# A causal attention loop on one core: how the row maxima are formed, and where projection work stands between scores and products

## The chip, the cores and the metric

The kernel runs on one core of a Trainium2 chip. The metric is the device time of one execution in microseconds. TensorE is written PE (matmuls) and PEld (weight loads), VectorE DVE, ScalarE ACT, GpSimd POOL, and SyncE SP; in this kernel SP issues nearly all DMA transfers. [...]

## The reference, cut to what matters

The program is a decoder of two layers on 8 sequences of 256 tokens with 512 features. Six sublayers follow each other, each added to its input and normalised. Three of the six are causal attentions over 256 tokens, and only those are touched here:

```python
# first sublayer: "a", differential attention, 32 query heads of 16, 8 key heads, 4 value heads of 32
scores = einsum('bhqd,bhkd->bhqk', q, k) * HD ** (-0.5)
scores = where(causal, scores, finfo.min)
attn_out = einsum('bhqk,bhkd->bhqd', softmax(scores), v)
lambda_full = exp(sum(lambda_q1 * lambda_k1)) - exp(sum(lambda_q2 * lambda_k2)) + LAMBDA_INIT
attn = attn_out[:, 0::2] - lambda_full * attn_out[:, 1::2]
attn = attn * rsqrt(mean(attn * attn, -1) + EPS) * ln_w * (1 - LAMBDA_INIT)
return attn @ Wo.T
# fourth sublayer: "s", causal self attention, 16 heads of 32
# sixth sublayer: "r", causal attention, 16 query heads of 32, one key and one value of 32 per token,
#                 chosen by the largest of 16 gates
```

Between them lie a long convolution and a mixture of experts (after a), and a cross attention (between s and r). The softmax subtracts each row's maximum before the exponential.

## The kernel before, in words

All three attentions run through one function, `causal_attention`, with `prepare` (projections for a group of four token tiles) and `finish` (output projection, sum and norm of two token tiles) given by the caller. Inside it the order of PE, DVE, ACT and POOL instructions is the order in which the Python code emits them. PSUM tiles and SBUF tiles come from pools; a tile that is asked for again waits until the old contents were read.

The work is cut into slots `u`. A slot handles four heads of one sequence (32 rows of the PE array each); a sequence has 8 slots in a (`upb` = 8) and 4 in s and r, so a has 64 slots, s and r have 32 each. A slot's data passes three stages at different times:

- `maxima(u)`: twelve score matmuls (`ps_q`, L1140), three 128x128 blocks for each of four heads: queries 0 with keys 0, queries 1 with keys 0, queries 1 with keys 1. ACT copies the two diagonal blocks to SBUF (`diag`, L1149). DVE reduces the block below the diagonal straight out of PSUM (`neg`, L1151). POOL masks the diagonal blocks (L1153). A second DVE reduction over `diag` (L1162) is returned as a function and emitted later in the slot. After the last slot of a sequence `split` (L1169 to L1176) writes the maxima as three bf16 terms, and one slot later `turn` (L1184) transposes them on PE and ACT copies them (`negT`, L1192).
- `weights(u - upb)`: the transposed scores less the maxima (`ps_k`, L1205 and L1214), the exponential on ACT (`pT`, L1222), the mask on POOL (L1223) and POOL's sum of two blocks (L1233).
- `products(u - lag)` with `lag = upb + 1`, called by `sums(u)`: weights times values (`ps_pv`, L1248), their sums by a matmul with ones (L1258), reciprocal and product on DVE (L1266, L1272). In a, `gather` takes the place of L1272: even slots multiply (L367), odd slots use `nlam`, the negated lambda (L370), and POOL adds the two (`yT_b`, L371).

So `products` in slot u uses the weights made in slot u - 1. The scores and the transposed scores share one PSUM tile of four banks (`ps_sc`, one buffer). `ps_pv` has one buffer as well, and three one-bank tiles (tag "mm") serve all other matmuls.

Projection work fills PE's gaps. `prepare` puts pieces into `queue`, each step with a cost (0.86 for a matmul group `MM`, 0.45 for a transpose group `TR`) and each piece with the slot at which it is due. `finish` puts pieces into `after`. `fill(budget)` emits steps until less than 0.3 of the budget is left; `need(u)` emits all that is due by slot u, whatever it costs. Every slot has two fills, a short one and the rest. `at` also registers small things for a later slot's "start", "mid" or "end". Before, a slot's order is:

```python
diagonal = maxima(u)
...            # turn of the sequence before, in its first slot
sums(u)
diagonal()
...            # split, "mid" events, short fill
if u >= upb:
    weights(u - upb)
left = fill(left + rate - short)
```

In a, `finish` also normalises each head: squares on ACT (L462), sums on PE (`norms`, L436), then the power -1/2 on POOL over 128x16 (L446), widening on ACT (`widen`, L444), a transpose on PE (`scaled`, L453), a product on DVE (L459) and the output projection (`out_tile`, which ends in `add_norm_later`: sum L211 and statistics L145, L146 on DVE, `rstd` L140, L141 on POOL, and the last product L154 in a later slot). In s, the tokens of the next group come from the experts' sum (`combine`: L1066, L1075) and are normalised by "mid" events.

At the start of a, SP issues: four token tiles, the weights, the other twelve token tiles, four transfers of `filters` (10 MB, for the convolution), then `ln_w` (`lnw`, four times) and the four lambda vectors (`lv`), then the zero fills of two arrays in DRAM. DVE scales `wo` by `lnw` (L278) and forms `nlam` (L291 to L296).

Of the kernel before, what the change touches and what calls it, by code (L numbers as in the profile page):

```python
# [16 lines left out]
F32 = mybir.dt.float32  # L17
# [6 lines left out]
P = 128  # L24
# [25 lines left out]
def decoder_kernel(ctx: ExitStack, tc: tile.TileContext, a: dict, out: bass.AP):  # L50
# [184 lines left out]
    def diff_attention():  # L235
# [11 lines left out]
        for t in range(4):  # L247
            nc.sync.dma_start(
                out=wo[32 * t : 32 * t + 32],
                in_=a["L0_attn_Wo"][P * t : P * (t + 1), :].rearrange("(k d) c -> d k c", d=32),  # L250
            )
        load_x(range(TPG, NT))
# [22 lines left out]
        lnw = const.tile([P, 1], F32, tag="lnw", name="lnw")  # L275
        for i in range(4):
            nc.sync.dma_start(out=lnw[32 * i : 32 * (i + 1), :], in_=a["L0_attn_ln_w"].unsqueeze(1))
# [4 lines left out]
        lv = const.tile([P, 4, HD0], F32, tag="lv", name="lv")  # L282
        for i, n in enumerate(("q1", "k1", "q2", "k2")):
            nc.sync.dma_start(
                out=lv[:, i, :],
                in_=a[f"L0_attn_lambda_{n}"].unsqueeze(0).broadcast_to([P, HD0]),
            )
# [137 lines left out]
        def finish(work, pools, t0, yT, at):  # L425

            cost = 2 * (0.4 + TR + KB * MM)
            if t0 == NT - 2:
                return cost
            wide = {}  # L430
            sq = squares(t0 // 2)

            def norms(i):
                ps = pools.tile([P, H0], F32, tag="mm", name="ps_ss")
                for k in range(KB):
                    nc.tensor.matmul(  # L436
                        ps[:, 4 * k : 4 * k + 4], lhsT=sq[:, k, i * P : (i + 1) * P], rhs=quad, start=True, stop=True
                    )
# [7 lines left out]
                at(0, "end", lambda: nc.gpsimd.tensor_tensor(rr, rr, neg_half, ALU.pow))  # L446
                at(1, "end", widen)
                at(2, "fill", [(TR, lambda: scaled(i))])
# [14 lines left out]
            for i in range(2):  # L463
                at(1 + i, "fill", [(0.4, lambda i=i: norms(i))])
# [621 lines left out]
    def causal_attention(name, prepare, finish, upb=KB, gather=None):  # L1086
# [18 lines left out]
        with ExitStack() as st:  # L1105
# [26 lines left out]
            def maxima(u):  # L1132
# [4 lines left out]
                for j, (i, keys) in enumerate(((0, 0), (1, 0), (1, 1))):  # L1137
# [10 lines left out]
                d = work.tile([P, 4, 2, P], F32, tag="diag", name="diag")  # L1148
                nc.scalar.copy(d, block[:, :, 0:3:2, :])  # L1149
                dst = neg[u // upb % 2][:, :, :, c]  # L1150
                nc.vector.tensor_reduce(dst[:, 1], block[:, :, 1, :], AX.X, ALU.max, negate=True)  # L1151
                rows = d.rearrange("p s j k -> p (s j) k")
# [10 lines left out]
                    dst[:, 0:3:2].rearrange("p j s -> p s j"), d, AX.X, ALU.max, negate=True  # L1163
# [173 lines left out]
            for u in range(units + lag + 2):  # L1337
# [499 lines left out]
```

## Time and profile before

| | |
|---|---|
| median of 3 runs | 2288.14 us (2285.28 to 2297.55) |
| profiled execution, its time | 2304.89 us |
| profiled execution, span from first to last instruction | 2303.1 us |
| mean granted TensorE clock | 0.957 |
| PE, DVE, POOL, ACT busy | 2078.3, 1282.2, 814.5, 545.9 us |
| scores of a, first to last | 21.2 to 486.0 us |
| scores of s and r, first to last | 1229.1 to 2259.4 us |

The views used below come from this one execution. A row of a timeline has the start and the duration in us, the engine, the source line, the operation with out<-in and its shape; in square brackets stands the idle time of the engine before it and what ended it. In a row of waits stand the waiting instruction, what it waited for, the total in us, the number of times and the longest. A row of groups ends in total busy time, mean ns of one, and idle time before it.

### The profile page before, as it was taken

The numbers are of one execution on the slowest core, as the hardware profiler recorded it, in microseconds if no ns is written. First come the engines' busy times: TensorE is split into PE (matmuls) and PEld (weight loads), VectorE is DVE, ScalarE is ACT, GpSimd is POOL, SyncE is SP. The second block draws the span as 40 slices with busy tenths as digits, with TensorE's granted clock in tenths as the row PEclk, the third lists the DMA queues.
The fourth block names the chain that finished last, engine by engine and source line by source line (L and its number), as shares of the span: only waits on it lengthen the run. The fifth ranks groups of instructions, "written<-read, shape, count | busy, mean of one in ns | idle before, by whom it ended". The sixth has DMA issues, their size and how long they took to land. (4 is left out here: it accounts for less than half of the span.)

```text
span 2303.1 us, 35720 instructions
## 1 busy us (share of the span) xinstructions
PE 2078.3 (90%) x14904; PEld 1200.5 (52%) x14904; DVE 1282.2 (56%) x2051; ACT 545.9 (24%) x723; POOL 814.5 (35%) x904
## 2 busy tenths in 40 slices
PE   7688888888999999899978999998999999999995
PEld 4344444544445346555543444444877876545443
DVE  3556666665888895122224556456343433577767
ACT  3334334431001003211112333331101101233322
POOL 2456556564654843000013444334000000133433
PEclk9899989989999999999988999999999999999998
DMA  7899601312413306213122111002001000000000
GB/s 241 307 384 384 240 2 38 98 45 55 179 28 114 115 23 222 80 62 135 60 108 76 38 37 56 19 1 93 28 10 37 28 10 1 1 10 10 15 15 29
DMA packets 110033, 197.57 MB, mean 86 GB/s; under 512 B 7088, under 2 KB 30768, under 8 KB 109872
## 3 DMA queue, kind: packets, MB, share of 16 engines
q1 hardware_dynamic: 104752, 178.49, 22.3%
q0 software_dynamic: 5120, 16.78, 2.2%
q8 instruction: 120, 1.97, 0.3%
q14 instruction: 41, 0.34, 0.0%
HBM read 93.54 MB, written 112.20 MB: 89 GB/s over the span
## 5 line engine op out<-in xcount | busy, mean ns | idle before, releaser
L171 PE MATMUL ps_y<-kv,wt 128*128 128x512 f32 x640 | 281.0, 597 | 4.6 <-POOL kv L508 3.7
L1222 ACT ACTIVATE pT<-ps_k 128x1536 f32<-128x1536 f32 x128 | 185.8, 1451 | 360.4 <-PE ps_k L1214 352.7
L1266 DVE RECIPROCAL rsum<-ps_pv 128x256 f32<-128x256 f32 x128 | 224.3, 1753 | 73.3 <-PE ps_pv L1258 73.3
L1151 DVE TENSOR_REDUCE neg<-ps_q 128x4 f32<-128x512 f32 x128 | 88.4, 691 | 311.7 <-ACT diag L1149 311.6
L1223 POOL TENSOR_SCALAR_AFFINE_SELECT pT<-pT 128x1024 f32<-128x1024 f32 x128 | 140.2, 1095 | 275.4 <-ACT pT L1222 275.1
L1153 POOL TENSOR_SCALAR_AFFINE_SELECT diag<-diag 128x1024 f32<-128x1024 f32 x128 | 140.0, 1094 | 186.3 <-ACT diag L1149 186.2
L171 PEld LDWEIGHTS ps_y<-kv,wt 128*128 128x128 f32 x640 | 120.2, 191 | 153.7 <-issue 135.7
L1149 ACT COPY diag<-ps_q 128x1024 f32<-128x1024 f32 x128 | 129.7, 1013 | 188.8 <-PE ps_q L1140 171.0
L1162 DVE TENSOR_REDUCE neg<-diag 128x8 f32<-128x1024 f32 x128 | 155.3, 1213 | 26.1 <-POOL diag L1153 26.0
L1233 POOL TENSOR_TENSOR pT<-pT 128x512 f32<-128x512 f32 x112 | 142.6, 1274 | 9.3
L140 POOL TENSOR_SCALAR rstd<-bn_mv 128x1 f32<-128x1 f32 x80 | 16.9, 211 | 322.1 <-DVE bn_mv L146 317.8
L1066 POOL DMA_INDIRECT w_l1x<-ys,slots x32 | 31.5, 983 | 280.2 <-DMA ys<-y_m 272.2
L182 PE MATMUL ps_f<-xT,w_l1a 128*128 128x512 f32 x256 | 121.1, 617 | 3.0 <-ACT xT L195 3.0
L182 PE MATMUL ps_t<-w_l1f,xT 128*128 128x512 f32 x256 | 121.5, 613 | 1.4 <-DVE sel L1654 1.4
L981 PE MATMUL po_m<-dn,hT 128*128 (+1 forms) x216 | 104.4, 621 | 12.0 <-ACT hT L974 10.5
L1258 PE MATMUL ps_pv<-pT,ones_v 128*32 128x256 f32 (+1 forms) x1152 | 88.9, 392 | 22.7 <-POOL pT L1233 22.4
L546 DVE TENSOR_REDUCE yc<-z 128x64 f32<-128x512 f32 x128 | 86.1, 674 | 6.1 <-POOL w_l1a L547 5.7
L1248 PE MATMUL ps_pv<-pT,v 128*32 128x256 f32 (+1 forms) x1024 | 60.0, 356 | 30.1 <-POOL pT L1223 29.4
L1205 PE MATMUL ps_k<-qT,kz 32*128 32x256 f32 (+1 forms) x1024 | 75.4, 382 | 4.5 <-DVE neg L1151 4.2
L1140 PEld LDWEIGHTS ps_q<-kT,qT 32*128 32x128 f32 x1536 | 49.2, 188 | 57.3 <-issue 31.6
L1140 PEld LDWEIGHTS ps_q<-kz,qT 32*128 32x128 f32 x1536 | 49.9, 190 | 55.7 <-ACT pT L1222 35.1
L182 PEld LDWEIGHTS ps_f<-xT,w_l1a 128*128 128x128 f32 x256 | 47.3, 194 | 59.5 <-issue 54.8
(327 smaller groups left out, 3763.8 us busy)
## 6 DMA issues: line engine op xcount, KB each, us to landing
xs<-zero SPq DMA_DIRECT2D x8, 4352.0 KB
ys<-zero SPq DMA_DIRECT2D x8, 4352.0 KB
filters<-in_L_xattn_k SPq DMA_DIRECT2D x4, 2560.0 KB
first_h<-xs SPq DMA_DIRECT2D x36, 256.0 KB
ys<-y_m SPq DMA_DIRECT2D x36, 256.0 KB
gu<-in_L_ffn_gate_up_proj SPq DMA_DIRECT2D x3, 2816.0 KB
wt<-filters SPq DMA_DIRECT2D x32, 256.0 KB
x<-in_x SPq DMA_DIRECT2D x16, 256.0 KB
```

Source lines behind the costliest of these rows:

```text
L171: nc.tensor.matmul(ps, lhsT=lhsT(k), rhs=rhs(k), start=(k == 0), stop=(k == n - 1))
L182: nc.tensor.matmul(ps[0], lhsT=lhsT(k), rhs=rhs(k), start=(k == 0), stop=(k == KB - 1))
L981: nc.tensor.matmul(po, lhsT=hT[:m, i, :], rhs=dn[i][:m, bass.ds(e, 1), :], start=(i == 0), stop=(i == len(FCH) - 1),)
L1140: nc.tensor.matmul(block[:, s, j, :], lhsT=q(rows, c, b * S + i * P, P), rhs=k(rows, c, b * S + keys * P, P), start=True, stop=True,)
L1149: nc.scalar.copy(d, block[:, :, 0:3:2, :])
L1153: nc.gpsimd.affine_select(out=rows, in_=rows, compare_op=ALU.is_ge, fill=-FAR, base=0, pattern=[[0, 8], [-1, P]], channel_multiplier=1,)
L1162: return lambda: nc.vector.tensor_reduce(dst[:, 0:3:2].rearrange("p j s -> p s j"), d, AX.X, ALU.max, negate=True)
L1222: nc.scalar.activation(p[:, 0:3].rearrange("p j s q -> p s j q"), block, AF.Exp)
L1223: nc.gpsimd.affine_select(out=p[:, 0:2].rearrange("p j s q -> p (j s) q"), in_=p[:, 0:2].rearrange("p j s q -> p (j s) q"), compare_op=ALU ...
L1233: nc.gpsimd.tensor_tensor(p[:, 3], p[:, 1], p[:, 2], ALU.add)
L1258: nc.tensor.matmul(ps[32 * s : 32 * s + 32, 1, j * P :], lhsT=ones_v, rhs=p[:, 1, s, :] if j else first[:, :, s, :], start=(j == 0), stop= ...
L1266: nc.vector.reciprocal(r, ps[:, 1, :])
```

## The change

It has five parts.

1. In `maxima`, ACT copies all three blocks to SBUF (`rows`, 128x1536), ordered so that the two diagonal ones lie together; POOL masks those two as before; one DVE reduction over all three is emitted later in the slot. The reduction out of PSUM is gone. The tile has two buffers in a and one in s and r (`diag` had two everywhere).
2. The short fill moves up: it now stands right after the scores, before `turn`, the products and the reduction.
3. The rest of the fill stops one `MM` early; then `need(u + 1)` emits what is due in the next slot; then the last step follows.
4. In a, the power over 16 columns is cut into two over 8, emitted at the ends of two slots; the second tile's `norms` comes two slots after the first's, and `widen` and `scaled` move accordingly. In the last-but-one sequence they stay as close as before.
5. The transfers of `lnw` and `lv` are issued before the twelve token tiles and the filters. The turn of the last sequence comes after the products of the following slot.

```diff
+        lnw = const.tile([P, 1], F32, tag="lnw", name="lnw")
+        for i in range(4):
+            nc.sync.dma_start(out=lnw[32 * i : 32 * (i + 1), :], in_=a["L0_attn_ln_w"].unsqueeze(1))
+        lv = const.tile([P, 4, HD0], F32, tag="lv", name="lv")
...
         load_x(range(TPG, NT))
         spread_filters()
...
-        lnw = const.tile([P, 1], F32, tag="lnw", name="lnw")
...
+            apart = 1 if t0 == NT - 4 else 2
...
-                at(0, "end", lambda: nc.gpsimd.tensor_tensor(rr, rr, neg_half, ALU.pow))
-                at(1, "end", widen)
-                at(2, "fill", [(TR, lambda: scaled(i))])
+                def root(half):
+                    r = rr[:, 8 * half : 8 * half + 8]
+                    nc.gpsimd.tensor_tensor(r, r, neg_half[:, :8], ALU.pow)
+
+                for half in range(2):
+                    at(half * (apart - 1), "end", lambda half=half: root(half))
+                at(apart, "end", widen)
+                at(apart + 1, "fill", [(TR, lambda: scaled(i))])
...
-                at(1 + i, "fill", [(0.4, lambda i=i: norms(i))])
+                at(1 + apart * i, "fill", [(0.4, lambda i=i: norms(i))])
...
-                for j, (i, keys) in enumerate(((0, 0), (1, 0), (1, 1))):
+                for j, (i, keys) in enumerate(((0, 0), (1, 1), (1, 0))):
...
-                d = work.tile([P, 4, 2, P], F32, tag="diag", name="diag")
-                nc.scalar.copy(d, block[:, :, 0:3:2, :])
-                dst = neg[u // upb % 2][:, :, :, c]
-                nc.vector.tensor_reduce(dst[:, 1], block[:, :, 1, :], AX.X, ALU.max, negate=True)
-                rows = d.rearrange("p s j k -> p (s j) k")
+                d = work.tile([P, 3, 4, P], F32, tag="rows", name="rows", bufs=2 if gather else 1)
+                nc.scalar.copy(d.rearrange("p j s k -> p s j k"), block)
+                rows = d[:, 0:2].rearrange("p j s k -> p (j s) k")
...
                 return lambda: nc.vector.tensor_reduce(
-                    dst[:, 0:3:2].rearrange("p j s -> p s j"), d, AX.X, ALU.max, negate=True
+                    neg[u // upb % 2][:, :, :, c], d, AX.X, ALU.max, negate=True
                 )
...
                 if u >= units:
 
+                    if u == units:
+                        sums(u)
+                        turn(B - 1)
                     if u < units + upb:
                         weights(u - upb)
-                    sums(u)
+                    if u > units:
+                        sums(u)
...
-                diagonal = maxima(u)
-                if u and u % upb == 0:
-                    turn(u // upb - 1)
-                sums(u)
-                diagonal()
-                if u % upb == upb - 1:
-                    split(u // upb)
-                happen("mid")
+                largest = maxima(u)
                 if u % upg == upb and u // upg + 1 < NG:
                     per_group = begin(u // upg + 1)
                 short = min(0.3 * rate, 0.8)
                 if rate > 2.7:
                     short += (rate - 2.7) / 2
                 left = fill(left + short)
+                if u and u % upb == 0:
+                    turn(u // upb - 1)
+                sums(u)
+                largest()
+                if u % upb == upb - 1:
+                    split(u // upb)
+                happen("mid")
                 if u >= upb:
                     weights(u - upb)
-                left = fill(left + rate - short)
-                if u == units - 1:
-                    turn(u // upb)
+                left = fill(left + rate - short - MM)
+
+                need(u + 1)
+                left = fill(left + MM)
                 happen("end")
```

More of the change, by code (lines that the diff above doesn't have):

```diff
@@ L251, in diff_attention @@
             )
+        lnw = const.tile([P, 1], F32, tag="lnw", name="lnw")
+        for i in range(4):
+            nc.sync.dma_start(out=lnw[32 * i : 32 * (i + 1), :], in_=a["L0_attn_ln_w"].unsqueeze(1))
+        lv = const.tile([P, 4, HD0], F32, tag="lv", name="lv")
+        for i, n in enumerate(("q1", "k1", "q2", "k2")):
+            nc.sync.dma_start(
+                out=lv[:, i, :],
+                in_=a[f"L0_attn_lambda_{n}"].unsqueeze(0).broadcast_to([P, HD0]),
+            )
         load_x(range(TPG, NT))
@@ L273, in diff_attention @@
         nc.vector.tensor_reduce(quad, ident.rearrange("p (t d) -> p t d", t=4), AX.X, ALU.add)
-        lnw = const.tile([P, 1], F32, tag="lnw", name="lnw")
-        for i in range(4):
-            nc.sync.dma_start(out=lnw[32 * i : 32 * (i + 1), :], in_=a["L0_attn_ln_w"].unsqueeze(1))
         nc.vector.tensor_scalar(
@@ L280, in diff_attention @@
         )
[L282 to L287, printed above, removed]
         lam = const.tile([P, 4], F32, tag="lam", name="lam")
```

## The prediction

> **What bounds the kernel now.** I read the page first, for the busiest engine and its clock.
>
> ```profile
> PE 2078.3 (90%) x14904; PEld 1200.5 (52%) x14904; DVE 1282.2 (56%) x2051; ACT 545.9 (24%) x723; POOL 814.5 (35%) x904
> ...
> PEclk9899989989999999999988999999999999999998
> ```
>
> TensorE (PE) is busy for 2078 of 2303 us, so time is won where PE stands still or runs at a lowered clock. Next the stretches of the three causal attentions (columns: length, then busy time and count of PE, PEld, DVE, ACT, POOL, then granted clock, DMA share, GB/s). I call them a (64 slots), s and r (32 slots each).
>
> ```profile
> 88.00:485.00 397.00, 338.69 (x4262) 192.15 (x4260) 253.67 (x308) 163.31 (x172) 234.83 (x213) 0.93 0.56 199
> ...
> 1229.00:1555.00 326.00, 307.53 (x2580) 149.51 (x2580) 178.43 (x262) 106.11 (x124) 138.66 (x154) 0.99 0.11 33
> ...
> 1967.00:2259.00 292.00, 274.25 (x2616) 145.30 (x2620) 203.14 (x305) 89.23 (x98) 104.01 (x108) 0.98 0.03 10
> ```
>
> In a, PE idles 58 us of 397 and its clock is 0.93; in s and r it idles 18 us each at almost full clock. So most of the room is in a. Third, PE's own waits over the whole run (us in total, times, longest):
>
> ```profile
> PE ps_pv L1248 <- POOL pT L1223: 47.3, 34, 11.5
> PE ps_n L1184 <- DVE terms L1173: 28.4, 11, 4.8
> PE ps_pv L1258 <- POOL pT L1233: 22.4, 47, 0.6
> ...
> PE ps_q L1140 <- ACT kT L1387: 7.6, 11, 0.7
> PE ps_k L1205 <- DVE neg L1151: 6.5, 9, 1.9
> ```
>
> The change aims at these five. A slot of a in the timeline shows the first and the third:
>
> ```profile
> 100.11 1.45 ACT L1222 ACTIVATE pT<-ps_k 128x1536 f32<-128x1536 f32 x1 [3.77 <-PE ps_k L1214]
> ...
> 101.61 0.95 PE L1140 MATMUL ps_q<-kz,qT 32*128 32x128 f32 x24 [0.57 <-ACT pT L1222]
> 101.62 1.09 POOL L1223 TENSOR_SCALAR_AFFINE_SELECT pT<-pT 128x1024 f32<-128x1024 f32 x1 [3.38 <-ACT pT L1222]
> ...
> 102.77 0.86 PE L1248 MATMUL ps_pv<-pT,v 128*32 128x256 f32 x16 [0.21 <-POOL pT L1223]
> ...
> 104.12 0.64 PE L1258 MATMUL ps_pv<-pT,ones_v 128*32 128x256 f32 x8 [0.50 <-POOL pT L1233]
> ```
>
> Products of slot u use the weights of slot u-1: exponential, POOL's select, POOL's add. Only the scores stand between, so PE waits 0.21 and 0.50.
>
> **The change, part by part.** Each sum is made on the profiled execution (2304.9 us; median of the runs 2288.1).
>
> *Lambda first.* The only long stall:
>
> ```profile
> 77.45 1.29 DVE L278 TENSOR_SCALAR w_l<-w_l,lnw 128x2048 f32<-128x2048 f32 x1 [9.25 <-DMA lv<-in_L_attn_lambda_q]
> ...
> 82.51 1.51 PE L1248 MATMUL ps_pv<-pT,v 128*32 128x256 f32 x16 [11.47 <-POOL pT L1223]
> ```
>
> DVE stands behind eight tiny transfers queued after the 10 MB of filters; POOL's add and select stand behind DVE, PE behind POOL. Moved ahead of 12 token loads, they land long before DVE's first reduction at 23 us. Gone: 11.47 us and the slow matmuls after it (1.51 for 0.86, 1.08 for 0.64, 1.24 for 0.71 and so on, 2.1 us). Late next: the usual 0.21 and 0.50. Net 12.9. On SP's queue eight issues of about 0.43 us delay the later token loads by 3.5 us; they are issued by 20.7 us and first turned at 52.3 us, so that costs nothing. The zero fills behind them start some 20 us earlier; the next load that a waits for is issued at 246 us.
>
> *A projection piece between scores and products.* The compiled order shows a piece there in 41 of a's slots 9 to 63 (in none before; it stood after the products), and in nearly every slot of s and r. A piece is 0.93 us on PE (1.98 for two), more than 0.21+0.50. The short waits of those 41 slots add up to 13.6 us in the PE timeline. On odd slots POOL first does `yT_b` (0.73), which waits for reciprocal 1.76 and L370 0.48, so a little returns: I take 11. The 14 slots without a piece keep theirs.
>
> In r the waits are 1.5 to 3.2 us long and have another cause:
>
> ```profile
> 2134.47 1.10 POOL L1223 TENSOR_SCALAR_AFFINE_SELECT pT<-pT 128x1024 f32<-128x1024 f32 x1
> ...
> 2135.62 0.86 PE L1248 MATMUL ps_pv<-pT,v_r 128*32 128x256 f32 x16 [1.46 <-POOL pT L1223]
> ```
>
> The exponential was over at 2131.2. POOL's queue held two `rstd` pairs first (to 2134.5), and these waited for DVE's residual and statistics, which stood behind reciprocal and reduction. These residuals come from an output piece in the short fill. Moved ahead of the products, that fill puts residual, statistics and `rstd` ahead of the reciprocal. I take all 11.2 us of r's waits, and the slow spell after the 3.21 one (2.2): 13.4. In s the norm is added by the "mid" event, still after products and reduction, so there the 1.76 and its like stay, 0.5 longer by the bigger reduction: 1 us lost.
>
> *Roots in halves.* L446 takes 2.92 us, L387 on half the columns 1.64. Two of L446 in a row:
>
> ```profile
> 141.97 5.83 POOL L446 TENSOR_TENSOR rr<-rr,neg_half 128x16 f32<-128x16 f32 x2
> ...
> 149.95 0.86 PE L1248 MATMUL ps_pv<-pT,v 128*32 128x256 f32 x16 [2.12 <-POOL pT L1223]
> ...
> 153.86 1.24 PE L1205 MATMUL ps_k<-qT,kz 32*128 32x256 f32 x8
> ```
>
> Four such waits in a: 2.12, 2.14, 2.65, 1.27, together 8.2. In halves, at most 3.3 us fall between two slots and a piece covers 0.93; one us stays, 7.2 gained. POOL pays 14 x (2 x 1.64 - 2.92) = 5 us of its own time, beside PE. After three of them matmuls run slow: the slots' PE time exceeds that of like slots by 2.0, 2.0 and 4.5, so 8.5 more. [...] The row above shows 1.24 us for what takes 0.71, 4 us after a gap of 2.12. I take the row[...].
>
> *All maxima to SBUF.*
>
> ```profile
> L1162 DVE TENSOR_REDUCE neg<-diag 128x8 f32<-128x1024 f32 x128 | 155.3, 1213 | 26.1 <-POOL diag L1153 26.0
> ...
> L1149 ACT COPY diag<-ps_q 128x1024 f32<-128x1024 f32 x128 | 129.7, 1013 | 188.8 <-PE ps_q L1140 171.0
> ...
> L1151 DVE TENSOR_REDUCE neg<-ps_q 128x4 f32<-128x512 f32 x128 | 88.4, 691 | 311.7 <-ACT diag L1149 311.6
> ```
>
> The copy grows by half; L1222 moves the same 1536 columns in the same layout in 1.45, so +0.44 a slot, 56 us on ACT (24% busy). One reduction takes the place of two: 512 columns more cost 1213-691, so 1.74 for 1.90, 21 us less on DVE. Score PSUM is now freed by the copy, at 1.07+1.45 = 2.5 us after the scores' start. The transposed scores (`ps_k`) come after 0.95+0.86+0.57 = 2.4 us, or 3.3 with a piece. So the 6.5 us of L1205 on `neg` go, 0.5 stays: 6.0. If that cover went, the copy would cost up to 128 x 0.44 = 56. I take nothing.
>
> *Due pieces a product ahead.* `ps_q` waits 7.6, 3.7 and 2.9 us for ACT's evacuations of kT and qT, 0.7 each time. A piece of 0.93 now stands between. I take 10 of 14.2; the cost of more reordering is nothing PE must do twice.
>
> *The turn after fill and, at the end, after products.* In a the turn waits for a chain on DVE: reciprocal, product, reduction, then six split operations. Rows show 0.18 to 0.23 us for these, or about 1.0 to 1.3 while POOL works. [...] So hiding 0.93 of the wait would by PE's order alone gain some 6 us in a's six inner turns. [...] it now starts a piece later and is 0.52 longer. For slot 39-40: the transposed scores came 11.9 us after slot 39's scores, and come at about 12.3. I take 0.4 x 6 = 2.5 lost. At the ends the last turn moves behind ready products (1.5 to 2.5 us of PE work): of the waits 2.82, 3.05 and 4.85 I take 8 back. Net 5.5.
>
> **Sum:** 12.9 + 11 + 13.4 - 1 + 7.2 + 8.5 + 6.0 + 10 + 5.5 = 73.5 us. From the profiled 2304.9 that makes 2231; the profiled execution lies 16.8 above the median, most likely in slow spells, so against the median: 2288.1 - 73 = 2215. About 45 of it is in a.
>
> **The rivals.** (0.5%, 11.4 us, is about what a measurement of this kernel tells from no change.)
>
> *The loop stays the bound* (smaller gain). From `ps_k`'s end, exponential 1.6, select 1.1, add 1.3, ones 0.6 and `ps_k` 1.1 make 5.7 us a slot against 6.4 of PE work; queues behind `yT_b` or the norms could close that gap, and then the pieces only change place. Only lambda, roots without spells, `neg` and half the due pieces count: 12.9+7.2+6+5 = 31, so 2257. For it: 14 slots without a piece. Against it: slots with four matmul records of fill already wait for the add alone.
>
> *Full clock in a* (larger gain). At 0.93 over 397 us, 28 us of clock are missing there; I counted 10.6 of a's spells and leave the turns' (about 10). If the shorter gaps end these too, 90 to 105: 2190.
>
> *The single rows buffer* (slower). In s and r the tile has one buffer (before: two): the copy of slot u+1 waits for slot u's reduction, `ps_k` behind the copy, and PE behind that. In r at 2133 the reduction ended at 2141.0 and the next copy began at 2146.0: 5.0 us of room. The bigger reduction takes 0.5 of it and the pieces ahead of the reciprocal 2.8, so 1.6 is left. Where DVE runs later than that, each us is PE's. It turns the 73 into a loss from 2.8 us a slot over 64 slots (room 1.6, then 1.2 x 64 = 74); at 3.5 it is 2288 - 73 + 122 = 2337. Against it: before, `ps_k` waited for a reduction of its own slot, which is later in DVE's order.
>
> *It does not do what it says*: pieces run out and PE has the old order. The compiled order excludes it for s and r.
>
> **How the numbers follow.** My sum 0.63 (2185 to 2240), the loop 0.17 (2240 to 2270), full clock 0.09, no measurable change 0.07, slower 0.04. The range 2178 to 2258 leaves out about 0.2: the end of the larger gain, and those near or above no change. Faster 0.89, same 0.07, slower 0.04.
>
> **What would show it.** The 11.47 wait gone; PE on POOL's `pT` from 69.7 us to under 30; `ps_k` on `neg` and `ps_q` on kT near zero; the turn's wait still near 20 us; the copy at 1.45, the reduction at 1.74; clock in a 0.95 or more. Wrong if PE's waits for `pT` stay above 45, if `ps_k` waits for the copy, or if a shortens by less than 25 us.

## The result, and the profile after

The changed kernel takes 2255.53 us (median of 4 runs, 2248.47 to 2261.73) against 2287.40 us (4 runs, 2285.28 to 2297.55): a ratio of 0.985, 95% interval 0.9814 to 0.9885 (ratios here are of the means, the times are medians). It is 32 us faster; the sum had forecast 73. The profiled execution took 2256.86 us. Its page (engine, busy time, share of the span, instructions; then the granted clock in 40 slices):

```profile
PE 2072.2 (92%) x14904; PEld 1204.6 (53%) x14904; DVE 1272.1 (56%) x1923; ACT 600.0 (27%) x723; POOL 820.2 (36%) x918
...
PEclk8999999798999999999979999989999999998898
```

PE is as busy as before (2072 us): what went is idle time. Look also at the end of the clock row, where r lies: it shows two 8s in a row, where before there were only 9s until the last slice. PE's waits over the whole run (total us, times, longest):

```profile
PE ps_pv L1254 <- POOL pT L1229: 18.6, 17, 2.7
PE ps_n L1190 <- DVE terms L1179: 14.1, 8, 2.7
...
PE ps_pv L1264 <- POOL pT L1239: 9.9, 23, 0.8
PE ps_o L182 <- DVE yT_b L467: 9.3, 4, 4.3
...
PE pt_k L1681 <- DVE k L1676: 4.6, 2, 2.3
...
PE ps_n L1190 <- DVE sel L1665: 3.0, 1, 3.0
PE pt L194 <- DVE sel L1665: 2.7, 1, 2.7
```

By the waits alone the forecast looks met. Those for POOL's `pT` fell from 69.7 us to 18.6 + 9.9 = 28.5; `ps_k` on `neg` is gone, `ps_q` on kT and qT is down to three waits of 0.7 us; the copy takes 1.44 us and the reduction 1.75, as said (the whole-run rows of groups):

```profile
L1168 DVE TENSOR_REDUCE neg<-rows 128x12 f32<-128x1536 f32 x128 | 223.5, 1746 | 64.9 <-POOL rows L1159 64.9
L1157 ACT COPY rows<-ps_q 128x1536 f32<-128x1536 f32 x128 | 184.1, 1438 | 182.8 <-PE ps_q L1148 153.6 <-DVE neg L1168 17.7 <-DVE v_r L1671 4.3
```

But the table of waits shows new names too: `sel`, `k`, and `yT_b` of the output projection. And the windows of a, s and r (length, then busy and count of PE, PEld, DVE, ACT, POOL, then clock, DMA share, GB/s) show where the time did not come:

```profile
88.00:440.00 352.00, 305.55 (x4056) 179.64 (x4056) 233.83 (x246) 176.07 (x163) 228.64 (x214) 0.96 0.62 221
1177.00:1500.00 323.00, 306.11 (x2553) 148.84 (x2552) 175.95 (x227) 118.30 (x123) 137.33 (x153) 0.98 0.11 34
1914.00:2214.00 300.00, 285.79 (x2642) 155.23 (x2641) 203.84 (x275) 103.53 (x99) 105.28 (x108) 0.94 0.03 10
```

In a the clock rose from 0.93 to 0.96 and the idle time fell from 58 to 46 us. The window of r is 300 us long instead of 292 (from the first scores to the last 297 against 292): idle fell from 18 to 14, but the clock fell from 0.98 to 0.94.

To compare kernels I cut each profile at fixed marks. "a" runs from the first `ps_q` to the convolution's first `ps_y`, s from its first `ps_q` to the cross attention's first `ps_x`, r from that attention's last `ps_x` to the end. The last column adds up, in slices of 1 us from r's first scores to its last, how far the granted clock lay under 1 (slices under 0.9 only): time at half clock counts half.

| kernel (us) | a | s | r | r's clock loss |
|---|---|---|---|---|
| before, two profiles | 543.8, 546.5 | 411.1, 410.2 | 404.3, 407.6 | 6.8, 10.1 |
| changed, three profiles | 504.6, 503.9, 504.5 | 414.7, 413.9, 417.4 | 404.2, 403.1, 403.2 | 18.6, 15.2, 15.2 |
| E1 ahead in a alone | 504.0 | 417.1 | 406.7 | 12.0 |
| E2 fill behind | 533.9 | 417.4 | 406.6 | 11.9 |
| E3 old maxima | 497.9 | 407.6 | 399.9 | 8.4 |
| E4 due late | 498.5 | 413.9 | 400.4 | 10.1 |
| E6 old maxima, due late | 496.5 | 410.2 | 411.2 | 20.3 |
| E7 lambda late | 521.0 | 414.5 | 403.2 | 15.1 |
| E8 whole roots | 507.7 | 410.9 | 402.3 | 13.5 |
| E9 turn ahead in s, r | 500.4 | 430.2 | 399.2 | 8.5 |
| E10 three edits | 496.8 | 418.3 | 406.6 | 11.9 |
| E11 turn first | 509.0 | 413.0 | 402.5 | 15.4 |
| E13 double rows | 503.5 | 417.6 | 405.8 | 15.2 |
| E14 best | 497.6 | 411.3 | 402.9 | 10.0 |
| E15 order alone | 507.6 | 408.6 | 411.8 | 17.0 |

So a gave 39 us (the sum had about 45 there), s lost 3 to 7 and r gave next to nothing, where the sum had 7 or 8 and some 20. In a, about half of the gain is clock: from the first scores to the last PE idles 56.5 us instead of 79.6, and its clock loses 20.5 us instead of 39.3 (35.8 in the second profile of before). A part of the profiles' difference, 47.9 us in the spans, is not the change's: the experts' stage between convolution and s took 362.8 us in the profile of before and 350.4 in that after. E12 below settles that.

### The profile page after: what moved, and what is told of

The parts are those of the page before. It is cut to its first block, busy times and chain, and to the rows that moved or that the text cites. A ratio compares the mean times of both kernels' runs of the same rounds, so it can differ in the third digit from the quotient of the medians.

```text
span 2255.2 us, 35573 instructions
## 1 busy us (share of the span) xinstructions
PE 2072.2 (92%) x14904; PEld 1204.6 (53%) x14904; DVE 1272.1 (56%) x1923; ACT 600.0 (27%) x723; POOL 820.2 (36%) x918
## 3 DMA queue, kind: packets, MB, share of 16 engines
q8 instruction: 120, 1.97, 0.4%
## 5 line engine op out<-in xcount | busy, mean ns | idle before, releaser
L1168 DVE TENSOR_REDUCE neg<-rows 128x12 f32<-128x1536 f32 x128 | 223.5, 1746 | 64.9 <-POOL rows L1159 64.9
L1157 ACT COPY rows<-ps_q 128x1536 f32<-128x1536 f32 x128 | 184.1, 1438 | 182.8 <-PE ps_q L1148 153.6
L1159 POOL TENSOR_SCALAR_AFFINE_SELECT rows<-rows 128x1024 f32<-128x1024 f32 x128 | 140.1, 1095 | 221.7 <-ACT rows L1157 221.0
L1074 POOL DMA_INDIRECT w_l1x<-ys,slots x32 | 31.5, 985 | 267.1 <-DMA ys<-y_m 259.2
L1264 PE MATMUL ps_pv<-pT,ones_v 128*32 128x256 f32 (+1 forms) x1152 | 88.9, 393 | 10.1 <-POOL pT L1239 9.9
L182 PE MATMUL ps_o<-w_l,yT_b 128*128 128x512 f32 x128 | 69.8, 660 | 9.9 <-DVE yT_b L467 9.3
L1148 PE MATMUL ps_q<-kz,qT 32*128 32x128 f32 x1536 | 63.3, 296 | 15.4 <-ACT pT L1228 11.8
L1211 PE MATMUL ps_k<-qT,kT 32*128 32x256 f32 (+1 forms) x1024 | 73.6, 374 | 3.9 <-ACT pT L1228 3.4
```

The source lines that it names most:

```text
L182: nc.tensor.matmul(ps[0], lhsT=lhsT(k), rhs=rhs(k), start=(k == 0), stop=(k == KB - 1))
L1148: nc.tensor.matmul(block[:, s, j, :], lhsT=q(rows, c, b * S + i * P, P), rhs=k(rows, c, b * S + keys * P, P), start=True, stop=True,)
L1157: nc.scalar.copy(d.rearrange("p j s k -> p s j k"), block)
L1159: nc.gpsimd.affine_select(out=rows, in_=rows, compare_op=ALU.is_ge, fill=-FAR, base=0, pattern=[[0, 8], [-1, P]], channel_multiplier=1,)
L1168: return lambda: nc.vector.tensor_reduce(neg[u // upb % 2][:, :, :, c], d, AX.X, ALU.max, negate=True)
L1264: nc.tensor.matmul(ps[32 * s : 32 * s + 32, 1, j * P :], lhsT=ones_v, rhs=p[:, 1, s, :] if j else first[:, :, s, :], start=(j == 0), stop= ...
```

## The experiments

Theories ahead of them. T1: the fill ahead of the products lets VectorE's chain (reciprocal, product, reduction, then the evacuations `sel` and `k`) start later, so at a sequence's end and start a tile of PSUM comes late, and PE's stop is followed by half clock. T2: the longer copy and reduction of the maxima cost what the order brings. T3: the pieces brought a product ahead collide. T4: nothing differs but the places at which the clock is low. In r, at the fourth sequence's start (slot 12), the timeline shows what T1 means, first before, then the changed kernel:

```profile
2071.29 0.29 PE L1184 MATMUL ps_n<-ident_b,terms 128*32 128x128 bf16 x8
...
2072.60 1.99 PE L194 MATMUL pt<-ident,x 128*128 128x128 f32 x16
2074.43 3.74 PE L171 MATMUL ps_g<-w_l1f,xT 128*128 128x16 f32 x32
```

```profile
2025.45 1.09 PE L194 MATMUL pt<-ident,x 128*128 128x128 f32 x8
2029.28 1.97 PE L194 MATMUL pt<-ident,x 128*128 128x128 f32 x8 [2.74 <-DVE sel L1665]
2031.04 6.84 PE L171 MATMUL ps_g<-w_l1f,xT 128*128 128x16 f32 x32
2037.82 0.40 PE L1190 MATMUL ps_n<-ident_b,terms 128*32 128x128 bf16 x8
2038.00 1.50 PE L1254 MATMUL ps_pv<-pT,v_r 128*32 128x256 f32 x16
```

Eight transposes take 1.09 us and the next eight, behind a wait of 2.74, 1.97; the 32 gate products then take 6.84 where before they took 3.74 (the granted clock was 0.50 from 2028.8 to 2042.4 us), and the turn, `ps_n`, stands behind all of it.

Kernels named E1 to E4, E5 to E8, E9 to E12 and E13 to E16 ran on one chip each, four chips in all.

### E1 and E2: where the short fill stands

```diff
# E1: ahead of the products in a only
+                if gather:
                     left = fill(left + short)
...
                 happen("mid")
+                if not gather:
+                    left = fill(left + short)
# E2: behind them everywhere
-                left = fill(left + short)
...
                 happen("mid")
+                left = fill(left + short)
```

> The short fill stands ahead of the products of probabilities only in a; in s and r it is behind them, as before the change. The changed kernel took 2255.5 us (median), with r at 404.4 us and s at 414.7. Theory T1 (in r and s the fill ahead of the products trades the waits for pT for late tiles of PSUM, each followed by a slow spell): PE's waits of ps_pv for POOL's pT come back in r (about 11 us), but the waits on sel and k at the ends of the sequences go and the clock in r rises from 0.94 to 0.97 or more, so r stays at 400 to 408 or gets shorter by 5 to 15 us: 2240 to 2258 in all. Theory T2 (the longer reduction and copy of maxima eat the gain of r): the order is worth what was forecast, so without it r gets longer by 10 to 13 us: 2265 to 2270. Theory T4 [...]: within 5 us of the changed kernel, with the clock's low slices at other places.

> The short fill is behind the products in all three attentions; all the rest is as changed. In a the waits of ps_pv for pT (23.5 us before, 7 to 10 after) come back: a gets longer by 10 to 15 us if the fill ahead of the products is worth there what the vanished waits say, by less than 4 if another wait took their place. With r and s as in the kernel that keeps the order in a alone. T1: 2255 to 2270 in all. T2: 2275 or more.

E1 took 2276.01 us (ratio to before on the same chip 0.9867, 0.9837 to 0.9897), E2 2301.91 (0.997, 0.9958 to 0.9983). The two differ only in a, by 25.9 us: the largest single effect of the study. A loss of 10 to 15 us had been expected. The windows of a's slots, first E2, then E1:

```profile
22.30:476.10 453.80, 380.95 (x4800) 217.20 (x4800) 269.98 (x280) 213.76 (x197) 261.01 (x242) 0.92 0.58 211
```

```profile
21.00:440.30 419.30, 362.51 (x4804) 213.57 (x4804) 271.76 (x280) 212.99 (x197) 260.53 (x242) 0.95 0.63 229
```

With the same matmuls, idle time falls from 72.9 to 56.8 us (16.1), and PE's busy time from 380.95 to 362.5 (18.4): more than half of the effect is clock, given back when the stops in between went. My sum had counted only the waits for this part. In s and r, E1 against the changed kernel's three profiles shows the order worth 0 to 3 us in s and 2.5 to 3.6 in r. T2 foretold 10 to 13 longer in r; that is refuted. T1 came true in part: with the old order the waits on `sel` and `k` in r fall from 10.3 us to 1.3, and r stays in T1's 400 to 408 us, but the clock does not recover: E1 loses 12 us there, at other places.

### E3, E4 and E6: maxima and due pieces as before

```diff
# E3
-                d = work.tile([P, 3, 4, P], F32, tag="rows", name="rows", bufs=2 if gather else 1)
-                nc.scalar.copy(d.rearrange("p j s k -> p s j k"), block)
+                d = work.tile([P, 4, 2, P], F32, tag="diag", name="diag")
+                nc.scalar.copy(d, block[:, :, 0:3:2, :])
+                nc.vector.tensor_reduce(dst[:, 1], block[:, :, 1, :], AX.X, ALU.max, negate=True)
# E4
-                left = fill(left + rate - short - MM)
-                need(u + 1)
-                left = fill(left + MM)
+                left = fill(left + rate - short)
# E6: both
```

> The maxima are taken as before: a copy of two of the three score tiles and two reductions, one of them from PSUM. T2 (the copy of 1536 columns on ScalarE and the single reduction of 1.74 us are what r lost): r gets shorter by 10 to 15 us, to about 392. T1: r stays at 400 to 408, since what holds the tiles is VectorE's whole chain and the old form takes as long on VectorE; in a the waits of ps_k for neg (11.5 us before) come back and a gets longer by 5 to 10 us: 2260 to 2266 in all.

> Due pieces are no longer put a product ahead: the rest of a slot's fill runs in one, and pieces that must be done are forced at the end as before. T3 (pieces brought ahead are what collides in s and r: pt_k waits for k on VectorE, 4.6 us, and the waits on sel 5.7 us with their slow spells): s and r get shorter by 3 to 6 us each, a longer by 5 to 10: 2252 to 2262 in all. T1: r and s stay within 3 us; a gets longer by 10 us, the term that I gave to this part: 2263 to 2268.

> The old form of the maxima and the late due pieces together. In the profiles the one alone shortened a by 6.6 us (504.6 to 497.9), s by 7 and r by 4.5; the other a by 6, s by 1 and r by 4. If they cost independently: 25 to 29 us below the changed kernel, a ratio of 0.973 to 0.975. If both cost the same thing (work put ahead of the products and of the reduction that holds tiles and VectorE), the gain of the two is that of one: 0.977 to 0.980. If neither edit matters and only the chip differs: as the changed kernel on this chip.

E3 took 2259.91 us (ratio 0.9784, 0.9758 to 0.9810), E4 2259.64 (0.9783, 0.9760 to 0.9807), both about 16 below E1 on that chip; E6 on the next chip 2253.38 (0.9822, 0.9797 to 0.9846) beside 2256.00 for the changed kernel. So either alone looks like a gain, both together hardly more than none. In E3 a did not get longer, though the waits of `ps_k` for `neg` came back with 13.7 us over the whole run (4.3 in a). In E4 the wait of `ps_q` for kT came back in full:

```profile
PE ps_q L1148 <- ACT kT L1395: 7.6, 11, 0.7
```

and a's slots were still no longer (416.5 us against 419.2 to 419.9). So taking this wait away won nothing that a's length shows. E6 has the shortest a but one of the longest r, 411.2, with 20.3 us of clock lost. In r, E3 and E4 keep most of the waits on `sel` and `k` (9.2 and 8.4 us), yet lose only 8.4 and 10.1 us of clock, no more than before: these waits do not by themselves decide the clock's loss. What the maxima cost in s is in the groups of its slots, E3 first, then the changed kernel once more (E5):

```profile
L1170 DVE TENSOR_REDUCE neg<-diag 128x8 f32<-128x1024 f32 x31 | 37.6, 1214 | 12.7 <-POOL diag L1161 12.7
...
L1157 ACT COPY diag<-ps_q 128x1024 f32<-128x1024 f32 x31 | 31.4, 1012 | 42.9 <-PE ps_q L1148 40.6 <-remote 1.9 <-DVE bn_st L145 0.3
```

```profile
L1168 DVE TENSOR_REDUCE neg<-rows 128x12 f32<-128x1536 f32 x31 | 54.2, 1748 | 37.4 <-POOL rows L1159 37.4
L1157 ACT COPY rows<-ps_q 128x1536 f32<-128x1536 f32 x31 | 44.6, 1439 | 45.8 <-PE ps_q L1148 37.4 <-DVE neg L1168 8.4
```

The chain from scores to maxima is copy, select (1.09 in both), reduction: 1.01 + 1.09 + 1.21 = 3.32 us before, 1.44 + 1.09 + 1.75 = 4.28 now. ScalarE and VectorE have time for it, but it is 0.96 us later for all that stands behind the reduction on VectorE. The 8.4 us of ScalarE are the single buffer; E13 tests that.

### E5, E7, E8: the changed kernel again; lambda and the roots undone

```diff
# E7: the transfers of lnw and lv back behind spread_filters()
# E8
-            apart = 1 if t0 == NT - 4 else 2
+            apart = 1
-                for half in range(2):
-                    at(half * (apart - 1), "end", lambda half=half: root(half))
+                at(0, "end", lambda: nc.gpsimd.tensor_tensor(rr, rr, neg_half, ALU.pow))
```

> The changed kernel once more, with nothing edited, to stand beside the others on the same chip. If the gain of 1.5% is the change's own, the ratio is 0.982 to 0.989 here too. If the old form of the maxima and the late due pieces (0.978 each, on another chip than the first runs) owed their ratio to that chip and not to their edits, the changed kernel shows 0.977 to 0.980 here.

> Only the loads of lambda and of the norm's weights go back behind the filters' loads. My sum gave this part 12.9 us: 2268 against 2255.5 of the changed kernel, with PE's wait of 11.5 us of ps_pv for pT back in the first slots. Rival: the first slots are bound by the loads of the weights anyway and the lost cover shows elsewhere: within 4 us.

> The roots are one pow of 16 columns again, at the old spacing. My sum gave this part 15.7 us (7.2 of waits for pT behind POOL and 8.5 of slow spells after them): 2271. Rival: with the fill ahead of the products PE has work while POOL takes the long pow, and the halves only make ps_o wait for yT_b (9.3 us, not there before): 2250 to 2258.

The changed kernel: 2256.00 us, 0.9839 (0.9813 to 0.9866). Without lambda first 2271.96, 16.0 longer (0.9903, 0.9877 to 0.9929), with its stall back as the longest of the first row:

```profile
PE ps_pv L1254 <- POOL pT L1229: 33.2, 17, 15.2
```

With whole roots 2260.81 (0.9863, 0.9836 to 0.9891), 4.8 longer where 15.7 was forecast; the intervals overlap. The windows of a's slots, the changed kernel (E5), then E8:

```profile
21.40:440.60 419.20, 362.50 (x4800) 213.66 (x4800) 271.64 (x280) 212.88 (x197) 260.10 (x242) 0.95 0.63 229
```

```profile
21.80:446.90 425.10, 373.62 (x4810) 218.87 (x4810) 277.83 (x284) 213.09 (x197) 256.81 (x232) 0.94 0.62 226
```

Idle time is 5.2 us higher with the halves (56.7 against 51.5; 56.2 to 57.5 in all other profiles of a as changed), and busy time is 11.1 us lower. Of that, 6.8 is clock (20.5 us lost against 27.3), and this is not told from luck: E11, with the halves, loses 29.0 in the same slots (last section). With whole roots PE's waits for `pT` come to 29.9 us, against 28.5 with the halves; what rises is the turn's wait for `terms`, from 14 us to 21:

```profile
PE ps_n L1189 <- DVE terms L1178: 21.0, 11, 3.3
...
PE ps_pv L1253 <- POOL pT L1228: 19.8, 15, 2.8
...
PE ps_pv L1263 <- POOL pT L1238: 10.1, 23, 0.8
```

The wait of `ps_o` for `yT_b` (9.3 us) is there with the halves and all but missing with whole roots (0.6 us): with the halves the output projection comes a slot later, and its input with it.

### E9 and E10: the turn ahead of the fill in s and r

```diff
# E9, and E10 with E6's edits as well
+                turning = not gather and u and u % upb == 0
+                if not turning:
                     left = fill(left + short)
                 if u and u % upb == 0:
                     turn(u // upb - 1)
                 sums(u)
+                if turning:
+                    left = fill(left + short)
```

> In s and r alone, the first slot of a sequence has the turn and the products ahead of the short fill, as before the change; all other slots keep the fill ahead. In the changed kernel those slots of r (4, 12, 20) hold waits of 2.7 and 3.0 us on sel and most of the 15 to 18 us that the clock loses in r's slots. T1 (work put ahead of turn and products at the sequence's start collides with VectorE's chain, and the stops bring half clock): the waits on sel go, the clock's loss in r's slots falls to 8 us or less, r is 390 to 397 us (404.4 and 403.1 in the two profiles of the changed kernel), s 2 to 5 shorter: 2240 to 2250 in all. T4 (the half clock comes with the gate products of 16 columns and the transposes, wherever they stand): r 400 to 406, 2252 to 2258 in all.

> The old form of the maxima, the late due pieces, and turn and products first at a sequence's start in s and r, together: the version that the experiments so far point to. If T1 is right: a about 496, s 405 to 410, r 390 to 397: 2230 to 2240 in all. [...]

E9 took 2278.31 us (0.9891, 0.9867 to 0.9915), E10 2266.42 (0.9831, 0.9809 to 0.9853): the first is slower than the changed kernel (0.984 to 0.985; the intervals just meet), the second not told from it. In r's slots E9 looks like what T1 said: the waits on `sel` went, the clock's loss fell to 8.5 us, and the slots took 289.0 us against 294.4 to 296.9. Windows of E9, s's slots and r's:

```profile
1185.70:1529.30 343.60, 318.21 (x2586) 153.96 (x2586) 177.98 (x231) 119.25 (x123) 139.13 (x156) 0.96 0.10 32
1941.20:2230.20 289.00, 273.57 (x2615) 146.58 (x2615) 206.90 (x274) 102.59 (x97) 104.16 (x108) 0.97 0.03 10
```

Two things speak against it. The waits only changed their name: in r's slots the turn now waits for `terms`, where the changed kernel waits 0.5 us,

```profile
PE ps_n L1190 <- DVE terms L1179: 8.7, 4, 3.5
```

and PE idles 15.4 us, against 13.4. And the gain did not come again: with the same edit r's slots took 296 us in E10 and 293 in E14 (clock's loss 11.9 and 10.0).

In s the same edit cost 14 to 17 us (343.6 against 326.2 to 329.4), where 2 to 5 of gain were expected. There the fill had been covering the turn's wait for `terms` and the products' wait for `pT`: three of the sequences' first slots show stops of over 4 us each. So the changed order serves s; whether it hurts r is not shown.

### E11 and E12: the last turn, and the kernel before once more

```diff
# E11
-                    if u == units:
-                        sums(u)
-                        turn(B - 1)
...
+                if u == units - 1:
+                    turn(u // upb)
```

> Only the turn of the last sequence goes back to the end of the last slot of scores. My sum gave the turn 5.5 us (8 at the ends of s and r, less 2.5 in a): 2261. Rival: the later turn shortens r's end (tail of 40 to 42 us against 44 before) and lengthens s's (88 against 85), and comes to nothing: 2253 to 2258, with s's tail at 85 and r's at 44.

> The kernel before once more, for its profile on this chip. In the profile of before and in the four of one chip the stage between the long convolution and s took 361 to 365 us, with one wait of 10.5 us of po_m for hT; in the changed kernel's and in the four of another chip 350 without it. If that is the chip's or the execution's doing and not the change's, the kernel before shows on a chip the same of the two as the changed kernels beside it.

E11 took 2272.58 us (0.9846, 0.9824 to 0.9869), the changed kernel's own ratio. Its ends, from the last scores on, are 87.1 us in s and 41.8 in r; the changed kernel's are 87.7 to 88.5 and 40.4 to 42.2. The turn's place at the ends is worth nothing. (Its later place inside a, for which the sum took off 2.5 us, was not tested alone.) E11's a is 5 us longer, which its edit cannot explain (see the last section).

E12's single run took 2313.0 us; the median of before beside it was 2305.67. Its experts' stage took 363.6 us, with the wait of the page of before:

```profile
PE po_m L981 <- ACT hT L974: 10.2, 1, 10.2
```

On the chips of E1 to E4 and of E9 to E12 that stage takes 359.6 to 364.7 us in every kernel, changed or not; on the two others 349.2 to 350.3 in every kernel, the order alone on the kernel before (E15) among them. So 12 us of the two first profiles' difference go with the chip, and ratios are only taken against the kernel before on the same chip.

### E13 to E16: double buffer, the best version, the order alone

```diff
# E13
-                d = work.tile([P, 3, 4, P], F32, tag="rows", name="rows", bufs=2 if gather else 1)
+                d = work.tile([P, 3, 4, P], F32, tag="rows", name="rows", bufs=2)
...
-                r = work.tile([P, S], F32, tag="rsum", name="rsum")
+                if gather:
+                    r = work.tile([P, S], F32, tag="rsum", name="rsum")
+                else:
+                    r = p[:, 3, 0:2, :].rearrange("p s q -> p (s q)")
# E14: E3's edit, and E9's with
+                turning = name == "r" and u and u % upb == 0
# E15: the kernel before with its short fill moved
                 diagonal = maxima(u)
+                left = fill(left + short)
...
                 happen("mid")
-                left = fill(left + short)
```

> The copy of the maxima has two buffers in s and r as well (the reciprocal goes into the used tile of probabilities there, to make room). In s of the changed kernel ScalarE stands 8.4 us for VectorE's reduction to free the one buffer, and the old form of the maxima shortened s's slots from 326.2 to 320.5 us. If the single buffer costs that: s's slots 320 to 322 here, 2248 to 2251 in all. If it is the chain from the scores to the maxima, longer by 0.96 us (copy 1.44, select 1.09, reduction 1.75 against 1.01, 1.09, 1.21): s's slots 325 to 327, as in the changed kernel.

> The old form of the maxima, and in r alone the turn and the products first at a sequence's start. From the profiles: a 498 to 502, s 408, r 394 to 400: 8 to 14 us below the changed kernel on the same chip. [...]

> The kernel before, with only the short fill moved between the scores and the products. My sum gave this part 11 us in a, 13.4 in r and -1 in s: 23 us, a ratio of 0.990. From the kernel with the fill behind the products against the one with it ahead in a alone (30 us in a, 3 in s, 2 to 4 in r): 35 us, 0.985, and most of the whole gain. If its worth hangs on lambda and the roots being out of the way: 0.990 to 0.994.

> The changed kernel, unedited, on the same chip as the double buffer and the version with the old maxima: ratio 0.982 to 0.987, with the clock's loss in r's slots at 15 to 19 us as in its two other profiles.

The changed kernel (E16): 2258.26 us, 0.9852 (0.9824 to 0.9881). With two buffers (E13) 2261.29 (0.9878, 0.9848 to 0.9908), s's slots 329.5 us against 329.4, though ScalarE's wait of 8.4 us on the reduction is gone: the single buffer costs nothing. The order alone (E15): 2265.97, 0.9886 (0.9858 to 0.9914), 23.3 us below before. That is my 23 in sum, and by luck: in the profiles it is 36 to 39 us less in a, 2 less in s, and 4 to 7.5 more in r. (The profiles differ by more than the medians because both of before were slow for their kernel, the first by 5 us beyond the chip's 12, E12's by 7, and E15's was 3.5 us fast.) Window of E15's r:

```profile
1917.30:2215.80 298.50, 283.36 (x2624) 152.58 (x2628) 210.80 (x305) 89.55 (x97) 104.47 (x108) 0.94 0.03 10
```

Idle time is 15.1 us against 17.8 in the window of before, but busy time is 283.4 against 274.3, at a clock of 0.94. With nothing else changed, r's gain is taken back through the clock (17.0 us lost against 6.8 and 10.1).

E14 took 2247.15 us, 0.9808 (0.9782 to 0.9833), and beats both kernels: its runs (2244.78 to 2249.55) all lie below those of the changed kernel beside it (2252.20 to 2262.03), 11.1 us in the medians, about what can be told here. By stages a is 6.9 us shorter, s 6.1 and r 0.3. Since the other edit touches r alone, a and s show what the new form of the maxima costs. In s's slots 4.1 us of it are idle time (12.3 against 16.4). In a the idle time differs by 1.0 us and the clock's loss by 3.4; but the four profiles of the changed kernel with the old form (E3, E6, E10, E14) lose 13.7 to 17.1 us of clock in a's slots, the ten with the new form in the same order 18.8 to 29.0.

## Why the prediction was right or wrong

The waits that the change aimed at went nearly as forecast, and 32 us came in place of 73. The terms for r's waits, the roots, the maxima, the due pieces and the turn were put too high; the term for the order in a was put too low.

- **Lambda first**, 12.9 forecast: 16.0. Right, stall and place.
- **A piece between scores and products.** In a 11 forecast: 25.9 in time, 30 in the profile. The waits named did go; the term was mis-sized because I counted the short waits and not the half clock that came and went with them (18 of 34 us of slot time). In r 13.4 forecast: next to nothing (the order as changed is worth 2.5 to 3.6 against E1; done alone it loses 4 to 7.5). The failed step is "I take all 11.2 us of r's waits": the `pT` waits went, but 2.7 + 3.0 + 4.6 us on `sel` and `k` took their place (before, 2.4 on `sel`), so r's slots idle only 4.3 us less, and the clock lost 15 to 18.6 us in place of 6.8 to 10.1. Why the clock lost more stays open: E9, E10 and E14 are rid of the waits on `sel` and lose 8.5 to 11.9 us, but E3, E4, E6 and E15 keep them and lose 8.4, 10.1, 20.3 and 17.0. In s, -1 was forecast; the order alone brings 2.
- **Roots in halves**, 15.7 forecast: 4.8, and not told from nothing. The step that failed is adding the waits and the slow spells as if no piece stood ahead of the products; with the piece there, whole roots (E8) add 1.4 us to the waits for `pT` and not 7.2, and with the halves `ps_o` is late by 9.3 us. That slow spells can follow gaps of 2 to 3 us was read rightly: in the first profile of before the clock was 0.50 from 151.8 to 155.1 us, after the gap of 2.12 us that ended at 149.95, and in the changed kernel's first half clock begins at the gap of 2.74 us above. They need not follow (last section), and of the 8.5 us put on them at most 6.8 came, not told from luck.
- **All maxima to SBUF**, 6.0 forecast: a loss of about 11 (E14 against E16; its r share, with E14's other edit, is 0.3). Both durations were met. The failed step is "I take nothing" for the copy: I priced engine time and the freeing of PSUM, and put at nothing that the maxima are ready 0.96 us later, on the engine whose queue holds `terms`, reciprocals and evacuations. The rival of the single buffer is refuted by E13. That the 0.96 us is the whole cause is argued from the rows; no run shortened the chain by itself.
- **Due pieces a product ahead**, 10 forecast: none seen. The step that failed is "I take 10 of 14.2". E4 brings the 7.6 us of wait back and a is no longer. Whether they cost (E4) or not (a and s of E6 and E14 agree within 1.1 us) stays open; r's clock differs by more than the effect.
- **The turn**, 5.5 forecast: nothing (E11). The step that failed is "I take 8 back" at the ends. The 2.5 us taken off in a were my estimate that VectorE's chain sets the date, starting a piece (0.93 us) later and with a longer reduction (1.75 us against 1.21); no run shows them.
- **The sum of what was measured.** 16.0 + 25.9 + 3 to 7 in s and r + 4.8 - 11 makes 39 to 43, against 31 to 37 in the three comparisons. The forecast of a clock of 0.95 or more in a was right (0.96). That a as a whole came within 6 us of the sum is luck: too little for the order and too much for roots, maxima and due pieces. The rival "full clock in a" held in part: 15 to 19 us of clock came back in a's slots, where the sum had 10.6. The rival "the loop stays the bound" named 2257, close to the result, but for a reason that did not hold: the `pT` waits fell as the sum said. And of the 16.8 us by which the profiled execution of before lay over the median, put down to slow spells, about 12 are the experts' stage (E12).

## What to carry to other kernels

Where PE is as busy as here (90 to 92%), cost a reordering by what the stops do to the clock as well as by the stops (E2 against E1 in a: 18.4 us of busy time beside 16.1 of idle time), and ask which wait comes next on the engine whose chain is now started later: here VectorE's, at the ends of sequences. A copy that is free on its engine is not free if its result is waited for (the maxima, 0.96 us later here, went with a loss of about 11 us); follow the latency of the chain to its last reader. An order that helps in one loop should be tried in each loop that shares the code: here the same lines won 30 us in a and next to nothing in r, and the variant that shortened r's slots in one profile cost 14 us in s. When an edit removes a wait, look for the same time under another name.

## What the runs showed of the hardware

**Half clock comes in steps, and the same wait does not always bring it.** In the profiles the clock is either 1 or 0.5. The clock records of the first profile of before and of the first of the changed kernel hold 53 stretches at 0.5: but for the last of each, which ends with the record, they are 1, 2, 3, 4 or 8 steps of 3.413 us long, and in each profile all changes of the clock, over 2.2 ms, lie on one raster of such steps to within 4 ns. r's loss comes in pieces of about 1.7, 3.4, 5.1 or 6.8 us: one to four steps at 0.5. Up to a's last slot E11 and the changed kernel are one program. Around the fourth sequence's turn, first the changed kernel (E5), then E11:

```profile
210.80 0.30 PE L1190 MATMUL ps_n<-ident_b,terms 128*32 128x128 bf16 x8 [2.46 <-DVE terms L1179]
210.93 0.82 PE L1254 MATMUL ps_pv<-pT,v 128*32 128x256 f32 x16
211.57 0.61 PE L1264 MATMUL ps_pv<-pT,ones_v 128*32 128x256 f32 x8
```

```profile
212.05 0.41 PE L1190 MATMUL ps_n<-ident_b,terms 128*32 128x128 bf16 x8 [2.46 <-DVE terms L1179]
212.24 1.50 PE L1254 MATMUL ps_pv<-pT,v 128*32 128x256 f32 x16
213.52 1.07 PE L1264 MATMUL ps_pv<-pT,ones_v 128*32 128x256 f32 x8
```

The wait is 2.46 us in both; one is followed by full speed (a clock of 1.00 in every slice of 1 us from 210.4 to 218.4), the other by 6.8 us at half clock. Over a's slots the idle times agree (56.7 and 56.5 us) and the clock's loss is 20.5 against 29.0 us. What decides whether half clock follows a wait was not shown; no run set where a wait lies on the raster. So some 3 to 9 us of a stage are luck (9 here; r of the unedited changed kernel lost 15.2, 15.2 and 18.6), and an effect of that size needs both kernels on one chip, several runs of each, and the profile's idle and busy time told apart.

**A small VectorE operation took six times as long, 1.09 us against 0.18, when it started while GpSimd's sum ran.** The first operation of `split` in s, before and then in the changed kernel (E5):

```profile
L1169 DVE TENSOR_TENSOR neg<-neg 128x16 f32<-128x16 f32 x7 | 1.2, 175 | 0.2
```

```profile
L1175 DVE TENSOR_TENSOR neg<-neg 128x16 f32<-128x16 f32 x7 | 4.9, 694 | 0.2
```

The mean of 0.69 us mixes two lengths. Four of the seven took 1.08 to 1.09 us, three 0.18; one of each, with what POOL did:

```profile
1246.54 1.27 POOL L1239 TENSOR_TENSOR pT<-pT 128x512 f32<-128x512 f32 x1
1246.75 1.09 DVE L1175 TENSOR_TENSOR neg<-neg 128x16 f32<-128x16 f32 x1
```

```profile
1292.50 0.18 DVE L1175 TENSOR_TENSOR neg<-neg 128x16 f32<-128x16 f32 x1
```

The long ones start while POOL's sum runs and end 0.03 to 0.04 us after it; beside the short ones POOL does nothing. In the first profiles of before and of the changed kernel, 50 of the 288 operations of `split` took over 0.26 us (0.66 to 1.29), and every one of these had started inside a sum or a select of POOL. Eight that started inside POOL's indirect transfers (L1074) took 0.18 to 0.23. So the record points to what POOL runs at that moment and not to the place: another 0.9 us in the chain ahead of the turn each time. An operation with one input can be long too: a cast (L1179) that started with POOL's select at 99.41 us took 1.13 us in the latter, where the median is 0.18.
